# Attention and routed experts on one core: other batch groups, a closer pace of indirect DMAs, and a counted clock that goes on behind the last quad

## The chip, the cores and the metric

The kernel runs on one core of one Trainium2 chip. The core has five engines that each work through an instruction queue of their own, in order: TensorE (PE, matmuls; PEld is its weight load), VectorE (DVE), ScalarE (ACT), GpSimd (POOL) and SyncE (SP), which here only issues DMAs. The metric is the device time of the core in microseconds (us); less is faster.

## The reference, cut to what matters

One transformer block with adaptive layer norms, over 16 batches of 512 tokens of width 128, in float32:

```python
h = layernorm(x) * (1 + ca) + sa            # per batch, from L0_c
x = x + ga * attention(h)                   # 16 heads of 8, rotary, causal softmax, projection
h = layernorm(x) * (1 + cb) + sb
logits = h @ router_w.T + expert_bias       # 160 experts
top_w, top_idx = top_k(sigmoid(logits), 8)  # 8 of 160 experts a token, weights scaled to sum 2.5
routed = sum over the 8: top_w * (silu(h @ w_gate[e].T) @ w_down[e].T)
shared = silu(h @ w_gate_shared.T) @ w_down_shared.T
x = x + gb * (routed + shared)
```

So 8,192 tokens each go to 8 of 160 small experts (128 to 64 to 128).

## The kernel before, in words

**Two stages.** The first stage (`attend`, L1076, 64 head groups `gg`: 16 batches with 4 groups of 4 heads) does the attention. Beside it run, batch by batch, the preparation of a later batch (`prepare`, `rotate` L284, `values`), the projection, and the routing (`route` L519: layer norm, logits, top 8). The second stage runs the experts in *quads*.

**Groups of batches.** Batches are routed in groups, `GROUPS` (L36). When all batches of a group are routed, `place` (L601) counts how many of its tokens each pair of experts gets and gives every token and expert choice a slot in a table `xg` of that group in HBM. A group of b batches has 32b + 80 blocks of 128 slots, that is 8b + 20 quads of four blocks. The last 8 of them (6 for a group of one batch) are spare: they run inside a condition (`spare_quads`, L867) that every engine reads and that is false here. So 8b + 12 quads run for b > 1 and 22 for b = 1, 228 in all with the groups of before.

**Scatter and gather.** The token rows go into `xg` by indirect DMAs that POOL issues (`scattering`, L741): 32 a batch, 512 in all, each moving 128 rows of 512 bytes. A quad (`Quad`, L769) loads four blocks of `xg`, turns them on PE (`turn`), multiplies by the gate weights (`up`, after ACT and DVE copied them to `wq`), applies Silu on ACT (`su`), multiplies by the down weights (`down`) and writes `yg`. When all quads of a group are through, its results can be fetched back: `gathering` (L966) issues 32 indirect DMAs a batch, 512 in all, eight to a tile `got`; `combine` (L986) weighs and adds the eight rows on DVE and, at the end of a batch, sends the rows to `out`. Before a batch can be combined, `shared_expert` (L885) and `weights` (L919) must have run for it.

**What sets the order.** The kernel writes the order of every engine's queue by hand, by a *counted clock* (`Steps`, L1237). Each matmul adds its estimated time to `steps.now` (`mm`, `turned`); DVE and ACT work is followed beside it. Side work is a list of generators with due times; `steps.tick()` runs up to two steps that are due. A step that yields `LATER` comes back 3 counted us later. Nothing of this exists on the chip: it only decides in which order instructions enter the queues.

- Beside the attention, a `Pacer` (L1014) is called after each of the 14 items of a head group and lets one scatter into the queue for every `PACE` counted us, as long as a placed group has scatters left; it may catch up by four.
- In the loop over quads, `RATE` is added to `owed` at every turn, and as many indirect DMAs are issued, scatters first, then gathers. If there is none to issue, `owed` is set to 0.
- `paced` (L228) makes every indirect DMA wait for the PE instruction that was last in the order, and keeps POOL's own order.
- Behind the loop, the gathers that are left are issued one after the other (L1208). `add_up(2)` takes the results up as they are complete; if the shared expert or the weights of that batch are not there, it runs steps and moves the clock on until they are.

**What shares POOL's and SP's queues.** POOL does two elementwise steps for each of the two `rotate` calls of a batch and two for its shifted rows (`side`, L234), in the same queue as the indirect DMAs. In `rotate`, ACT's copy of the second part (L307) reads what POOL wrote, and SP's DMAs `parts<-three` (L316) wait for POOL's second step; `rows<-h` (L598) waits for POOL's steps on `h`. On SP's queue the same order also holds the rows `qrep<-mT` (L412) that each head group's scores need, the loads `krep`, `qrep` for a head group four ahead, and DMAs that clear `xg` and the spare part of `yg` (`clear`, L508); what is left of those at the end of the attention is issued ahead of the first quad's loads.

Of the kernel before, what the change touches and what calls it, by code (L numbers as in the profile page):

```python
# [32 lines left out]
E = 160  # L33
I = 64
NC = E * I // P
GROUPS = (2, 3, 3, 2, 2, 2, 1, 1)  # L36
TOPK = 8
FAR = 1e30
LAG = 3


PACE, RATE = 1.3, 2.3


AFTER, LATER, AHEAD, SLACK = 0.8, 3.0, 3.0, 3.0
# [7 lines left out]
def slot_blocks(batches):  # L53

    return TOPK * NBLK * batches + NC


NKM = slot_blocks(max(GROUPS))

# [11 lines left out]
def block_kernel(ctx: ExitStack, tc: tile.TileContext, t: dict, out: bass.AP):  # L71
# [22 lines left out]
    steps = Steps()  # L94
# [396 lines left out]

    somes = const.tile([1, len(GROUPS)], I32, tag="somes", name="somes")

    class Group:
        def __init__(self, g):
            self.g, self.size, self.first = g, GROUPS[g], sum(GROUPS[:g])
            self.tb = NBLK * self.size
            self.nk = slot_blocks(self.size)
            self.nq = self.nk // 4
            self.idx = sb.tile([P, self.tb, TOPK], I32, tag=f"idx{g}", name="idx")  # L500
            self.pid = sb.tile([1, self.nq, 9], I32, tag=f"pid{g}", name="pid")
            self.some = somes[:, g : g + 1]
            self.m, self.before = [], []
            self.hide = tc.dram_tile([2, self.nk * P], BF, name=f"hide{g}")
            self.xg = tc.dram_tile([self.nk * P, D], FP, name=f"xg{g}")
            self.yg = tc.dram_tile([self.nk * P, D], FP, name=f"yg{g}")
# [12 lines left out]
    def route(gr, i):  # L519
# [37 lines left out]
        for j in range(NBLK):  # L557
# [7 lines left out]
            if j % 2:  # L565
                yield
        m = sb.tile([P, NBLK, E], BF, tag="m", name="m", bufs=max(GROUPS) + 2)
        vec.tensor_scalar(m, marked, 0.0, None, ALU.is_gt)
# [3 lines left out]

        before = sb.tile([P, E], BF, tag="before", name="before", bufs=max(GROUPS) + 3)
        if i == 0:
            vec.memset(before, 0.0)
            gr.before.append(before)
            before = sb.tile([P, E], BF, tag="before", name="before", bufs=max(GROUPS) + 3)
        two = sb.tile([P, 2, E], BF, tag="two", name="two")
# [429 lines left out]
    def stream(*sources):  # L1008

        return next((s for s in map(next, sources) if s is not None), None)  # L1010
# [149 lines left out]
    def prepare_sums():  # L1160

        nonlocal shared_last, gathered_last
        if gathers:
            gathered_last = gathers[0][0].first + gathers[0][1]
        if shares and shares[0] <= gathered_last + 1 and (
            shared_last is None or shared_last in residual
        ):
            shared_last = shares.popleft()
            steps.add(1, shared_expert(shared_last))

    def add_up(most):
        while len(sums) > most:
            b = sums[0][0].first + sums[0][1]
            while b not in residual or residual[b][2] is None:
                prepare_sums()
                if not steps.tick():
                    steps.skip()
            combine(*sums.popleft())

    for i in range(-3, len(quads) + 5):  # L1180
# [25 lines left out]
            owed = owed - 1.0 if stream(scatter, gather) is not None else 0.0  # L1206
        add_up(LAG)
    while stream(gather) is not None:  # L1208
        steps.tick()
        add_up(2)  # L1210
        prepare_sums()
# [217 lines left out]
```

## Time and profile before

| what | value |
|---|---|
| median of 6 runs | 1999.51 us (1989.74 to 2006.53) |
| the profiled execution | 2014.3 us, span of its instructions 2012.5 us |
| PE busy | 1631.9 us, 81% of the span |
| DVE, ACT, POOL busy | 1181.6, 1080.5, 1143.7 us |
| scatters (`xg<-hs`) | 512, mean 970 ns |
| gathers (`got<-yg`) | 512, mean 1005 ns |
| attention: first issue of a scatter to last | 277.6 to 1284.8 us (the last 128 of them beside the quads) |
| quads: first and last result copy `y<-down` on ACT | 1035.9 and 1848.8 us |

The profile is one execution. Its page gives the busy time of every engine, 40 slices of the span with the busy share in tenths, the granted clock of PE, the chain of work that ended last, the costliest groups of instructions, and the DMA issues. Further answers of the trace are groups by tile, waits ("who waited for whom: us in total, times, longest"), the instructions in order of time, and the busy time of the engines in chosen windows. In waits a "q" behind an engine's name is its sequencer, and "issue" means that nothing else was waited for.

### The profile page before, as it was taken

The numbers are of one execution on the slowest core, as the hardware profiler recorded it, in microseconds if no ns is written. First come the engines' busy times: TensorE is split into PE (matmuls) and PEld (weight loads), VectorE is DVE, ScalarE is ACT, GpSimd is POOL, SyncE is SP. The second block draws the span as 40 slices with busy tenths as digits, with TensorE's granted clock in tenths as the row PEclk, the third lists the DMA queues.
The fourth block names the chain that finished last, engine by engine and source line by source line (L and its number), as shares of the span: only waits on it lengthen the run. The fifth ranks groups of instructions, "written<-read, shape, count | busy, mean of one in ns | idle before, by whom it ended". The sixth has DMA issues, their size and how long they took to land. (4 is left out here: it accounts for less than half of the span.)

```text
span 2012.5 us, 39282 instructions
## 1 busy us (share of the span) xinstructions
PE 1631.9 (81%) x12248; PEld 1117.0 (56%) x12248; DVE 1181.6 (59%) x3153; ACT 1080.5 (54%) x2031; POOL 1143.7 (57%) x1139
## 2 busy tenths in 40 slices
PE   2799999989999989898978899898888897987100
PEld 1455555555455545454457788776767776776000
DVE  2677777878777768777523324345555554455544
ACT  1366656656565545555656666565656565664000
POOL 4001147407773767776435576666666665666776
PEclk8799999999999989999989999989999898998555
DMA  3465656656675776767788899888888897987221
GB/s 88 115 185 179 183 170 208 201 170 198 201 229 177 228 218 210 229 202 227 254 269 281 264 311 311 277 279 283 286 282 278 271 303 247 301 294 234 85 67 54
DMA packets 298149, 445.30 MB, mean 221 GB/s; under 512 B 44923, under 2 KB 168796, under 8 KB 297920
## 3 DMA queue, kind: packets, MB, share of 16 engines
q1 hardware_dynamic: 265152, 375.32, 57.7%
q0 software_dynamic: 32768, 67.17, 11.5%
q8 instruction: 113, 1.85, 0.4%
q14 instruction: 116, 0.95, 0.1%
HBM read 223.37 MB, written 218.17 MB: 219 GB/s over the span
## 5 line engine op out<-in xcount | busy, mean ns | idle before, releaser
L974 POOL DMA_INDIRECT got<-yg,idx x512 | 514.5, 1005 | 262.9 <-issue 104.8
L751 POOL DMA_INDIRECT xg<-hs,idx x512 | 496.4, 970 | 273.7 <-PE s L104 111.5
L1232 DVE TENSOR_REDUCE mins<-s 128x2 f32<-128x1024 f32 (+3 forms) x448 | 396.1, 912 | 146.1 <-PE s L104 144.0
L1232 ACT ACTIVATE pT<-s 128x1024 f32<-128x1024 f32 x320 | 322.0, 1021 | 198.7 <-PE s L104 195.3
L104 PE MATMUL down<-wd,su 128*128 x1824 | 276.0, 297 | 32.6 <-ACT su L1232 10.1
L104 PEld LDWEIGHTS down<-wd,su 128*128 128x128 f32 x1824 | 232.3, 199 | 110.5 <-issue 44.6
L104 PE MATMUL up<-xT,wq 128*128 128x128 f32 x1824 | 256.7, 287 | 1.8 <-ACT xT L1232 1.8
L1232 DVE COPY wq<-wg 128x128 f32 x456 | 91.5, 252 | 257.4 <-PE up L104 183.7
L104 PEld LDWEIGHTS up<-xT,wq 128*128 128x128 f32 x1824 | 237.9, 204 | 1.9 <-issue 1.9
L1232 ACT COPY y<-down 128x512 f32<-128x512 f32 x228 | 133.8, 587 | 182.0 <-PE down L104 108.7
L104 PE MATMUL s<-krep,qrep 96*128 96x512 bf16 (+3 forms) x1024 | 198.9, 307 | 34.4 <-DMA qrep<-parts 22.2
L104 PE MATMUL s<-qrep,krep 128*128 128x512 bf16 (+3 forms) x1024 | 195.5, 304 | 34.9 <-ACT pT L1232 16.3
L104 PE MATMUL av<-pT,v 128*32 128x512 f32 (+3 forms) x2048 | 196.7, 451 | 0.0
L236 POOL TENSOR_TENSOR rot<-rot,three 128x512 f32<-128x512 f32 x32 | 36.7, 1161 | 273.7 <-ACT three L1232 273.4
L111 PE MATMUL turn<-ident,xs 128*128 128x128 f32 x912 | 148.7, 289 | 31.0 <-DMA xs<-xg 29.9
L104 PEld LDWEIGHTS <-identb 128*128 128x128 bf16 x1280 | 121.9, 99 | 84.6 <-issue 6.7
L1232 ACT ACTIVATE su<-up 128x512 f32<-128x512 f32 x228 | 136.4, 598 | 49.1 <-PE up L104 48.4
L104 PEld LDWEIGHTS <-qrep 96*128 96x128 bf16 x1024 | 82.5, 99 | 135.1 <-issue 100.1
L1232 ACT COPY xT<-turn 128x512 f32<-128x512 f32 x228 | 131.9, 579 | 27.3 <-issue 14.7
L111 PEld LDWEIGHTS turn<-ident,xs 128*128 128x128 f32 x912 | 112.3, 149 | 47.6 <-issue 29.0
L1232 ACT COPY wq<-wg 128x128 f32 x456 | 113.4, 296 | 43.1 <-issue 14.8
L104 PEld LDWEIGHTS <-krep 128*128 128x128 bf16 x1024 | 86.4, 98 | 77.8 <-issue 56.8
(174 smaller groups left out, 2202.1 us busy)
## 6 DMA issues: line engine op xcount, KB each, us to landing
xg<-zeros SPq DMA_DIRECT2D x288, 256.0 KB
xs<-xg SPq DMA_DIRECT2D x228, 256.0 KB
wd<-in_wdT SPq DMA_DIRECT2D x228, 256.0 KB
yg<-y SPq DMA_DIRECT2D x228, 256.0 KB
krep<-parts SPq DMA_DIRECT2D x64, 288.0 KB
qrep<-parts SPq DMA_DIRECT2D x192, 96.0 KB
yg<-zeros SPq DMA_DIRECT2D x60, 256.0 KB
parts<-three SPq DMA_DIRECT2D x96, 128.0 KB
```

The source lines that it names most:

```text
L104: steps.last = nc.tensor.matmul(out_, lhsT=lhsT, rhs=rhs, start=start, stop=stop).ins
L111: steps.last = nc.tensor.transpose(out_, in_, ident).ins
L236: in_order(getattr(nc.gpsimd, op)(*args).ins)
L751: s = nc.gpsimd.indirect_dma_start(out=gr.xg, out_offset=bass.IndirectOffsetOnAxis(ap=gr.idx[:, NBLK * i + j, k : k + 1], axis=0), in_=h[: ...
L974: s = nc.gpsimd.indirect_dma_start(out=got[:, k, :], out_offset=None, in_=gr.yg, in_offset=bass.IndirectOffsetOnAxis(ap=gr.idx[:, NBLK * i ...
L1232: return getattr(self.engine, op)(*args, **kwargs)
```

## The change

Four numbers change, and one line is added. The groups become 3, 3, 3, 2, 2, 1, 1, 1; the pace of the scatters beside the attention goes from 1.3 to 1.05 counted us; the indirect DMAs per turn of the quad loop go from 2.3 to 2.4; and behind the loop every gather now moves the counted clock on by 1.25, so that side steps become due between the gathers. From this follow other counts: 230 quads run instead of 228 (36 for each group of three batches, 28 for two, 22 for one), and 58 instead of 60 spare quads are cleared in `yg`.

```diff
-GROUPS = (2, 3, 3, 2, 2, 2, 1, 1)
+GROUPS = (3, 3, 3, 2, 2, 1, 1, 1)
...
-PACE, RATE = 1.3, 2.3
+PACE, RATE = 1.05, 2.4
+PERIOD = 1.25
...
     while stream(gather) is not None:
+        steps.work(PERIOD)
         steps.tick()
         add_up(2)
         prepare_sums()
```

Every line behind the numbers stands one or two lines lower in the changed kernel.

## The prediction

> **What bounds the kernel now.** I read the page's slices first, then windows by stage, then who waits for whom in each stage. The slices show two stages in which PE is nearly full, and an end in which POOL alone works:
>
> ```profile
> span 2012.5 us, 39282 instructions
> PE   2799999989999989898978899898888897987100
> POOL 4001147407773767776435576666666665666776
> PEclk8799999999999989999989999989999898998555
> ```
>
> The windows put numbers on it (PE, PEld, DVE, ACT and POOL busy, granted clock, DMA share, GB/s):
>
> ```profile
> 150.00:200.00 50.00, 47.74 (x396) 26.71 (x395) 37.84 (x81) 32.92 (x50) 7.09 (x6) 1.00 0.60 184
> 550.00:600.00 50.00, 46.79 (x382) 25.52 (x375) 36.84 (x81) 32.26 (x48) 37.53 (x37) 1.00 0.73 221
> 1600.00:1650.00 50.00, 45.73 (x331) 38.66 (x330) 26.69 (x77) 32.97 (x78) 35.00 (x36) 0.97 0.92 299
> 1950.00:2000.00 50.00, 0.00 (x0) 0.00 (x0) 23.46 (x53) 0.00 (x0) 38.12 (x40) 0.50 0.19 57
> ```
>
> Attention (to about 1001 us) and quads (to 1849) are PE's: 46 to 48 of 50 us. What POOL does there is hidden as long as nobody waits for it. The last 160 us are POOL's: 40 gathers in 50 us. The reader should see there that POOL has no hole to be filled; one gather follows the other every 1.25 us, and its waits from 1845 us on are issue time only:
>
> ```profile
> 1946.62 0.94 POOL L974 DMA_INDIRECT got<-yg,idx  x1 [0.30 <-issue]
> 1947.86 0.94 POOL L974 DMA_INDIRECT got<-yg,idx  x1 [0.30 <-issue]
> ...
> POOL got L974 <- issue: 33.8, 111, 0.3
> ```
>
> Beside the attention POOL has to serve two customers, and before the change it manages. The rows are the scatters of one group of three batches alone, all of POOL in the same window, and, from the waits of 60 to 1000 us, the wait of ACT for POOL's step in `rotate`:
>
> ```profile
> 455.00:603.00 148.00, 93.01 (x96) 0.99 0.68 211
> ...
> 455.00:603.00 148.00, 112.25 (x112) 0.99 0.68 211
> ...
> ACT three L1232 <- POOL rot L236: 2.5, 3, 1.4
> ```
>
> **The change part by part.** Sums are against the profiled span of 2012.5 us (2014.3 us in all, which is 0.7% above the median of 1999.51). A change below 0.5%, 10 us, is about what a measurement cannot tell from none.
>
> *Two quads more (36+36+36+28+28+22+22+22 = 230).* PE's part of a quad in the chain is 1.21 (up) + 1.09 (down) + 0.85 (turn) = 3.15 us. From the first to the last `y` copy, 1035.9 to 1848.8, a quad took 3.58 with the group ends, whose number does not change. Two cost 6.3 to 7.2; I take 7, PE being the bound.
>
> *The end.* In the order of POOL's instructions, 116 gathers stand behind the last group's condition before, 97 after. At 1.25 us that is 19 x 1.25 = -23.8 us. Some gathers beside the window's DVE work took up to 1.92; over the end the mean was 1.29, so the ends are -23.8 and -24.5. Why they are fewer: following the counted clock through the code, 397 instead of 384 scatters lie ahead of the end of the attention. Between there and the last condition lie 128 + 396 = 524 indirect DMAs before and 115 + 415 = 530 after: 2.30 a quad both times. The rate of 2.4 is eaten by turns that find nothing to issue while the 36 quads of the first group run, so the quads themselves carry no denser DMAs, and their pace should stay.
>
> *The clock behind the loop.* POOL waits for nothing in the end, so moving steps between the gathers can win nothing there: 0. It could lose: each gather waits for the PE instruction last in the order, now a shared-expert matmul that waits for `hr`, whose load stands on SP behind `out`, which waits for DVE. The nearest row, gathers waiting for such matmuls while quads still ran, was 41.0 us over 23 times, 6.2 the longest. Two batches are still to come there (14 and 15, one fewer than before): 0 to 12; I take 0, since their loads are issued 20 or more gathers (25 us) ahead of need or while quads run.
>
> *One more shared expert inside the quad loop* (batch 13, before in the end): PE runs of 1.00 and 1.08 us for its `o` matmuls in the chain, plus four transposes and one gate matmul: 0 to 4, I take 2.5.
>
> *Clears.* Ahead of the first quad's loads, SP issued 36 clears in 27.11 us, 0.75 each, and PE stood 16.4 us for them. Now 34: -1.5, or 0 if another load is last. The DMAs they move past are only those loads.
>
> *The closer pace.* In the window of 148 us, 96 scatters came every 1.54 us at 1.3 counted us, so a counted us is 1.19 us and the new pace asks for one every 1.25. POOL needs 0.96 + 0.30 = 1.26 for a scatter, and its side steps took 112.25 - 93.01 = 19.2 us in 148, 0.13 a us. For a group of three batches: asked in 96 x 1.25 = 120 us, needed 96 x 1.26 + 120 x 0.13 = 137. POOL falls 17 us behind by the end of the group; at the old pace, 148 against 121 + 19 = 140, it does not. Queued behind the scatters on POOL are the side steps: in the new order two `rot` steps behind 53 scatters of each large group (lag 9.4) and two behind all 96 (lag 17). ACT's copy of `three` stands 3 counted us later (3.6 us), so it holds ACT's queue, exponentials included, for 9.4 - 3.6 = 5.8 and 17 - 3.6 = 13.4 us; `parts<-three` and `rows<-h` hold SP's, and with it the `qrep<-mT` rows of the next head group. Those rows were issued 7 to 10 us ahead of their use mostly (344.37 for matmuls at 352.19). I take the near end of that margin, 7 us, as the cover of both: the first hold is hidden, the second costs 13.4 - 7 = 6.4, for three large groups 19. Bounds: 0 (all hidden) and 3 x 13.4 = 40. The next group has 64 scatters and a lag of 64/96 x 17 = 11; less 3.6 and 7 it costs nothing.
>
> A hold has a price behind it. PE stood 3.56 us at 357.0 and then ran at half clock:
>
> ```profile
> 354.00:358.00 4.00, 1.00 (x8) 0.99 0.72 210
> 358.00:361.00 3.00, 3.00 (x26) 0.50 0.56 166
> ```
>
> The clock record has 3.4 us for that stretch, so 1.7 us lost; for three holds 5 (0 to 10).
>
> The scatters' own row has a median of 960, a mean of 970 and a maximum of 1572 ns, beside a DVE that is busy 37 of 50 us. [...] By the row the stretch is 10 ns each, so the measurement decides, and the sum has nothing for it.
>
> *Sum:* 7 - 23.8 + 0 + 2.5 - 1.5 + 19 + 5 = +8.2 us on 2012.5. On the median: 1999.5 + 8 = 2008.
>
> **The rivals.**
>
> *The holds stay hidden.* For it: ACT is idle 18 of 50 us beside the attention, PE has three score banks ahead, and all its waits for `pT` come to 20.7 us in 918. Then 19 + 5 fall away: -15.8, 1984. Against it: ACT's queue is in order, and 13.4 us is more than three banks' exponentials of 1.02 us each.
>
> *The holds cost in full*, the mechanism that ends clearly slower: a lag of 17 with no cover but the 3.6 us. Three times 13.4 and 5 of half clock: 40 + 5 - 15.8 = +29, 2028. It decides from 3.6 us a group on, where 3 x 3.6 + 5 = 15.8 balances what is won; 0.5% slower needs 7. For it: the margin of `qrep<-mT` was 5.3 us in some head groups, and each lag hits ACT and SP one after the other. Against it: while PE stands, no scatter is released, so the lag stops growing.
>
> *The change does not do what it says.* The rate is no denser, as shown; if the pace too gave nothing (POOL saturated: scatters simply late), the end would still have the 97 gathers, since the order is fixed. What is left of this rival is that the scatters land as before and hold nobody: the hidden case again, with more or less of the 13 scatters' 13 x 1.25 = 16 us kept, 1984 to 2000.
>
> **How the numbers follow.** Partly covered holds (the sum) 0.50, own range -2 to +20 us, 1997 to 2019, about half of it above +10; hidden 0.22; full 0.25; the last 0.03. Predicted 2008. The range reaches from the hidden case to the full one, 1984 to 2028, and leaves out less than 2 in 10. Faster by over 0.5%: nearly all of the hidden case, 0.21. Slower by over 0.5%: the full case and almost half of the sum's, 0.48. Same: 0.31.
>
> **What would show it.** Holds: ACT `three` waiting for POOL `rot` for 20 us or more instead of 2.5, SP `parts` and `rows` for POOL too, PE gaps above 3 us with half clock behind them near the end of each large group's scatters, and the attention's end near 1025 instead of 1001. If the wait is there and the attention still ends by 1005, the first rival is right. The end: 97 gathers, last `y` copy to the end of the span near 139 us instead of 163 (2012.5 - 1849.4), POOL still without waits. Quads: 3.58 us each as before. Wrong would make it: gathers waiting for `o` matmuls in the end, another pace of the quads, or a clock that differs over a whole stage.

## The result and the profile after

The changed kernel took 2022.95 us (median of 20 runs) against 1998.21 us for the kernel before (46 runs): a ratio of 1.0116, 95% interval [1.0100, 1.0132]. The forecast was 2008 with a range from 1984 to 2028. Slower was right and the range held it, but the time lost is 25 us on the medians, three times the 8 us forecast.

Four experiments (e1 to e4) ran on a chip on which the kernel before takes 2205 us, all others on chips on which it takes 1996 to 2005; so every ratio below is to runs of the kernel before on the same chip. There is no profile of the kernel before on the slower chip; for its stages e1 to e4 are compared with each other.

The stages, read from the first and last exponential (`pT`) and the first and last `y` copy of each trace, in us. "Again" are the two kernels once more, both on one chip (e8 and e5):

| stage | before | after | before again | after again | forecast of the change |
|---|---|---|---|---|---|
| start to first `pT` | 81.9 | 81.3 | 82.6 | 82.3 | 0 |
| attention | 919.0 | 951.4 | 920.0 | 952.2 | +24 |
| last `pT` to first `y` | 35.6 | 44.4 | 37.9 | 39.7 | -1.5 |
| first to last `y` | 812.9 | 813.4 | 800.6 | 813.9 | +9.5 |
| last `y` to the end | 163.1 | 135.3 | 163.2 | 133.7 | -23.8 |
| span | 2012.5 | 2025.8 | 2004.4 | 2021.8 | +8.2 |

The slices of the changed kernel: the right end of PE's row is 9, 4, 0, 0 where it was 7, 1, 0, 0, and in the attention (slices 8 to 19) it has 8s and a 7 where mostly 9s stood. GpSimd (POOL) shows 7s there with valleys of 1 and 2 between the runs of scatters:

```profile
span 2025.8 us, 39393 instructions
PE   2799999887988898988949989988998989889400
POOL 4001114772577177775462546667666766566776
PEclk8899999998999999998978989989898989899655
```

The windows that answer to those of before (PE, PEld, DVE, ACT and POOL busy, granted clock, DMA share, GB/s). A stretch without scatters is as full as it was (47.74 of 50 us of PE); 550 to 600, in the middle of a large group's scatters, falls from 46.79 to 42.80. The quads and the end are what they were:

```profile
150.00:200.00 50.00, 47.74 (x411) 27.10 (x410) 38.16 (x91) 34.82 (x52) 7.09 (x6) 1.00 0.58 181
550.00:600.00 50.00, 42.80 (x335) 23.93 (x333) 35.58 (x88) 27.49 (x43) 39.20 (x41) 0.99 0.63 200
1600.00:1650.00 50.00, 45.59 (x331) 38.80 (x330) 30.87 (x85) 32.88 (x78) 37.91 (x38) 0.97 0.94 308
1950.00:2000.00 50.00, 0.00 (x0) 0.00 (x0) 20.46 (x47) 0.00 (x0) 37.77 (x40) 0.50 0.20 58
```

The 96 scatters of a large group now take 136 us instead of 148; the prediction worked out 137 as what GpSimd needs. The scatters alone in that window:

```profile
327.00:463.00 136.00, 92.98 (x96) 0.97 0.64 203
```

and all engines in it, where GpSimd's 106.79 us hold 13.8 of other steps:

```profile
327.00:463.00 136.00, 116.92 (x943) 64.09 (x942) 95.19 (x235) 74.25 (x113) 106.79 (x108) 0.97 0.64 203
```

And ACT stands for GpSimd's step of `rotate`: 46.4 us in 11 waits, 8.3 the longest, where it was 2.5 in 3 (waits from 60 us to the attention's end; total, times, longest):

```profile
ACT three L1234 <- POOL rot L237: 46.4, 11, 8.3
```

One of these holds in the timeline (start, duration; in brackets the idle time before it and what ended it). GpSimd comes from a scatter straight into the two `rot` steps; between them ACT gets the input it had waited 8.34 us for; behind that copy in ACT's queue stood `hT`, and PE waited 7.54 us for it:

```profile
460.23 0.96 POOL L752 DMA_INDIRECT xg<-hs,idx  x1 [0.30 <-issue]
461.21 2.27 POOL L237 TENSOR_TENSOR rot<-rot,three 128x512 f32<-128x512 f32 x2
462.40 0.62 ACT L1234 CAST three<-rot 128x512 bf16<-128x512 f32 x1 [8.34 <-POOL rot L237]
462.93 0.77 ACT L1234 ACTIVATE hT<-s,mod 128x512 f32<-128x512 f32 x1
...
463.75 1.01 PE L105 MATMUL s<-qrep,krep 128*128 128x128 bf16 x4 [7.54 <-ACT hT L1234]
```

The price behind it: PE was empty from 460 to 463, and then nearly full, but at half clock; the clock record has it until 476.5.

```profile
460.00:463.00 3.00, 0.00 (x0) 0.00 (x0) 0.00 (x0) 0.59 (x2) 2.75 (x3) 0.50 0.13 44
463.70:467.00 3.30, 3.25 (x20) 1.61 (x19) 0.49 (x1) 2.26 (x5) 3.22 (x3) 0.50 0.34 110
467.00:470.00 3.00, 3.00 (x16) 1.64 (x8) 0.80 (x2) 0.58 (x1) 1.25 (x2) 0.50 0.43 146
470.00:474.00 4.00, 4.00 (x17) 2.31 (x17) 0.79 (x1) 1.53 (x2) 0.00 (x0) 0.50 0.00 0
```

A hold of the group of two batches behind the three large ones, for which the prediction had no cost, with the copy 6.42 us late and PE's gap of 5.28 us behind it:

```profile
918.52 0.62 ACT L1234 CAST three<-rot 128x512 bf16<-128x512 f32 x1 [6.42 <-POOL rot L237]
...
919.46 0.90 PE L105 MATMUL s<-wroutT,hT 128*128 128x160 f32 x2 [5.28 <-ACT row L1234]
```

Over the attention PE's idle time went from 73.0 to 97.2 us and the time at half clock from 33.7 to 61.4 (again: 76.2 to 94.4, and 37.5 to 71.7). In the kernel before, eight `up` matmuls took 1.06 us at full clock and 1.91 at half (starting at 1307.99 and 1325.51 us); from that, half of the time in which PE is busy at half clock is put down as its cost, an estimate. PE was busy at it for 31.9 us before and 47.7 after, so 7.9 more (again 35.8 and 63.7, 14.0 more). Idle time and half clock together make 32.1 and 32.2 us, all of what the attention grew.

The end has 100 gathers behind the last `y` instead of 119, on average 1.27 us apart where it was 1.30, and GpSimd still waits for little but issue (3.2 us in 10 other waits):

```profile
POOL got L975 <- issue: 26.5, 87, 0.3
```

### The profile page after: what moved, and what is told of

It is laid out like the page before. It is cut to its first block, busy times and chain, and to the rows that moved or that the text cites. A ratio compares the mean times of both kernels' runs of the same rounds, so it can differ in the third digit from the quotient of the medians.

```text
span 2025.8 us, 39393 instructions
## 1 busy us (share of the span) xinstructions
PE 1646.2 (81%) x12289; PEld 1123.9 (55%) x12289; DVE 1171.5 (58%) x3156; ACT 1084.1 (54%) x2041; POOL 1137.4 (56%) x1139
## 3 DMA queue, kind: packets, MB, share of 16 engines
q8 instruction: 113, 1.85, 0.4%
## 5 line engine op out<-in xcount | busy, mean ns | idle before, releaser
L105 PE MATMUL down<-wd,su 128*128 x1840 | 277.3, 296 | 31.1 <-ACT su L1234 10.2
L237 POOL TENSOR_TENSOR rot<-rot,three 128x512 f32<-128x512 f32 x32 | 36.5, 1158 | 322.1 <-ACT three L1234 322.0
L1234 ACT ACTIVATE su<-up 128x512 f32<-128x512 f32 x230 | 137.6, 598 | 48.9 <-PE up L105 48.2
L1234 ACT COPY wq<-wg 128x128 f32 x460 | 114.6, 295 | 49.3 <-issue 13.8
```

Of the source, the lines that this page charges most:

```text
L105: steps.last = nc.tensor.matmul(out_, lhsT=lhsT, rhs=rhs, start=start, stop=stop).ins
L237: in_order(getattr(nc.gpsimd, op)(*args).ins)
L1234: return getattr(self.engine, op)(*args, **kwargs)
```

## The experiments

### One part alone, and the change without its pace

e1 is the changed kernel with one part undone; e2, e3 and e4 are the kernel before with one part of the change each.

```
e1, from the changed kernel          e2, from the kernel before
-PACE, RATE = 1.05, 2.4              -PACE, RATE = 1.3, 2.3
+PACE, RATE = 1.3, 2.4               +PACE, RATE = 1.05, 2.3

e3, from the kernel before           e4, from the kernel before
-PACE, RATE = 1.3, 2.3               -GROUPS = (2, 3, 3, 2, 2, 2, 1, 1)
+PACE, RATE = 1.3, 2.4               +GROUPS = (3, 3, 3, 2, 2, 1, 1, 1)
```

> The changed kernel with only the pace of the scatters put back to 1.3 counted us; groups 3,3,3,2,2,1,1,1, rate 2.4 and the counted clock behind the loop stay. Theory of the holds (scatters in POOL's queue hold the side steps that ACT and SP wait for): ACT's wait for POOL in rotate falls from 46.4 us to 3 or less, the attention ends at about 1001 instead of 1033 us, PE idle in it near 73 instead of 97 us, the end stays at 135 us: 1970 to 1985 us, 1 to 1.4% under the kernel before. Rival, the groups (a first group of three batches starts its scatters a batch later and moves routing work): the attention stays near 1030 and the time at 2015 to 2025.

> The kernel before with only the pace changed, 1.05 for 1.3 counted us. Theory of the holds: two large groups and two or three of 64 scatters fall within the attention; holds of ACT by POOL of 30 to 45 us in all, attention longer by 20 to 32 us, the end unchanged at 160 us or so: 2018 to 2030 us, 1.0 to 1.6% slower. Rival, the groups: no more than 5 us from 1998. Rival, denser scatters slow PE through the DMA queues and not through waits: slower by as much, but with ACT waiting for POOL under 5 us.

> The kernel before with only the rate changed, 2.4 for 2.3 indirect DMAs a turn of the quad loop. If the rate is what shortens the end: the order of instructions leaves about 21 gathers fewer behind the last condition, 21 x 1.25 = 26 us, quads unchanged: 1970 to 1975 us, 1.2 to 1.4% faster. If the prediction's reading is right, that the rate is eaten by empty turns and the pace fills the end: within 8 us of 1998. Rival, denser gathers beside the quads slow them: the end shorter by 26 us, the quads longer by as much, 1998.

> The kernel before with only the groups changed to 3,3,3,2,2,1,1,1. Two quads more at 3.5 us, the end unchanged or some gathers longer because the first gathers start later, no holds (ACT waiting for POOL in rotate 3 us or less): 1998 to 2012 us, same to 0.7% slower. If the groups carry the loss, 2018 or more, with the attention longer by 20 us or the first quad's loads later by 9 us as in the changed kernel.

| run | median us | ratio to before | 95% interval | attention | gathers behind the last `y` |
|---|---|---|---|---|---|
| e1 changed, pace 1.3 | 2200.22 | 0.9992 | [0.9964, 1.0020] | 1025.7 | 97 |
| e2 pace alone | 2263.83 | 1.0277 | [1.0223, 1.0331] | 1086.0 | 117 |
| e3 rate alone | 2193.07 | 0.9952 | [0.9927, 0.9977] | 1020.8 | 94 |
| e4 groups alone | 2212.52 | 1.0041 | [1.0012, 1.0069] | 1021.6 | 117 |

So on this chip the loss lies in the pace: alone it costs 2.8%, and without it the changed kernel is level with the one before. And the rate is not without effect, as the prediction had it: with the rate alone 94 gathers are left for the end, with pace or groups alone 117 (the kernel before leaves 119 on the other chips).

What e2 did not show was the wait. With a pace of 1.05 and the old groups, on this chip, ACT's wait for `rot` (60 to 1170 us) is the old one, and yet the attention is 65 us longer than in e3 and e4 (against e3, 31.5 us of PE's idle time and 35 of half clock):

```profile
ACT three L1232 <- POOL rot L236: 2.5, 3, 1.4
```

So a second theory had to be tested: that scatters in close succession slow the attention themselves, whoever waits for GpSimd.

### Both kernels again, ACT's copy later, the pace alone

e5 is the changed kernel and e8 the kernel before, unchanged; e7 is e2's kernel again; e6 is the changed kernel with this edit in `rotate`, so that ACT's next copy is put 4 counted us later into its queue:

```
-        yield side("tensor_tensor", r, r, three[:, 0, :], ALU.subtract)
+        yield side("tensor_tensor", r, r, three[:, 0, :], ALU.subtract) + 4.0
```

> The changed kernel once more, so that it stands beside its variants on one chip. If the parts of the change simply add up as the runs so far had them (pace +2.8%, rate -0.5%, groups +0.4%), 1.027 of the kernel before on a chip that runs the kernel before in 2205 us, and 1.012 on one that runs it in 1998 us.

> The changed kernel with ACT's first copy of three issued 4 counted us later behind POOL's step of rotate; the same scatters at the same pace. Theory A, the closer pace costs by ACT's queue being held for POOL's late steps: ACT's wait of three for POOL's rot falls from 46 us to below 20, PE's gaps of 5 to 8 us behind it go, and the attention is 15 to 30 us shorter than in the changed kernel, the time 0.988 to 0.995 of it. Theory B, scatters in close succession slow the attention whoever waits for POOL: the wait falls as well, but the attention keeps its length within 8 us, and the time stays within 0.4% of the changed kernel.

> The kernel before with the pace of 1.05 alone, once more, beside a profile of the kernel before on the same chip. There was no wait of three for POOL's rot in it, so by theory A (only the holds cost) it is within 0.5% of the kernel before on a chip where the kernel before takes 2000 us; by theory B it is 2% or more slower there too, as it was at 1.028 on the slower chip, with 15 us or more of PE's waits that are not for POOL.

> The kernel before, for its profile on this chip. If it is the chip of 2205 us, the blocks of four heads that have no scatters beside them take 51 and 53 us as on the first chip, and those with 35 to 42 scatters take 66 to 76 instead of 56 to 69; on the first chip the profile repeats itself within 1%.

| run | median us | ratio to before | 95% interval | attention | PE idle in it | half clock in it |
|---|---|---|---|---|---|---|
| e5 changed | 2021.67 | 1.0126 | [1.0094, 1.0159] | 952.2 | 94.4 | 71.7 |
| e6 changed, copy later | 2018.95 | 1.0117 | [1.0086, 1.0148] | 948.1 | 96.3 | 51.0 |
| e7 pace alone | 2028.33 | 1.0159 | [1.0122, 1.0196] | 946.3 | 91.7 | 64.8 |
| e8 before | 2006.2 (one run) | | | 920.0 | 76.2 | 37.5 |

On this chip the pace alone does make ACT wait, so the statement in e7's expectation that there was no such wait holds for the slower chip only. ACT's wait in e7 (60 to 1030 us):

```profile
ACT three L1232 <- POOL rot L236: 33.1, 10, 6.7
```

and two of PE's (81 to 1028 us), for tiles that stand behind `three` in ACT's queue; e8 has 0.6 us for `hT` and none for `row`:

```profile
PE s L104 <- ACT row L1232: 8.2, 2, 5.6
PE s L104 <- ACT hT L1232: 6.1, 3, 5.4
```

e6 is the instructive one. The edit does what it says: ACT's wait for GpSimd is back at 2.5 us. Yet the attention is only 4.1 us shorter than in e5 and the time 0.1% less. Theory A (the holds of ACT are the cost) wanted 15 to 30 us. What PE waited for in e6 (82 to 1030 us):

```profile
PE s L105 <- DVE mins L1234: 26.2, 47, 1.9
PE s L105 <- DMA qrep<-mT: 17.1, 7, 3.9
PE s L105 <- ACT pT L1234: 13.4, 24, 2.2
PE o L112 <- DVE hide L1234: 8.2, 9, 1.6
PE s L105 <- DMA qrep<-parts: 6.4, 3, 4.0
```

The waits for `pT`, `hT` and `row` went down from 48.9 us in e5 to 13.4; in their place PE waits 23.5 us for rows of the next head group (`qrep`, by DMA; 10.4 in e5, 4.5 in e8) and 26.2 for VectorE's `mins` (7.9 in e5, but 19.3 in e8 too). By this run alone, theory B has it: the time is B's. But there is a third reading, A2: what is late is GpSimd's step, and whichever way that lateness is passed on, through ACT's queue or through rows that the rest of the chain makes late, PE ends up waiting for it. One such chain stands in e6's timeline: behind its scatters GpSimd comes late to its steps on `h`, SP's `rows<-h` waits 10.0 us for them, the `qrep` rows stand right behind it on SP, and PE waits for these:

```profile
930.83 2.62 POOL L237 TENSOR_TENSOR h<-h,row 128x512 f32<-128x512 f32 x2
...
933.47 0.34 SPq L599 DMA_DIRECT2D rows<-h  x1
933.91 0.77 SPq L413 DMA_DIRECT2D qrep<-mT  x1
...
936.22 0.61 PE L105 MATMUL s<-qrep,krep 128*128 128x512 bf16 x1 [3.91 <-DMA qrep<-mT]
```

The lateness itself can be read in the trace, as the time from ACT's copy that feeds a `rot` step to the step's start: 12.1 to 15.3 us for 11 of the 13 late steps in the changed kernel (the other two 8.2 and 9.3), 6.4 to 11.4 for most in e6, at most 8.8 in e8.

### GpSimd's steps on VectorE

This separates A2 from B: scatters as close as before, but nothing of `rotate` behind them. In e9, e10 and e13, `side` (the two subtractions of `rotate` and the two steps on rows) is VectorE's:

```
 def side(op, *args):
-    in_order(getattr(nc.gpsimd, op)(*args).ins)
+    getattr(nc.vector, op)(*args)
     return LATER
```

e9 is the kernel before with this, e10 also has the pace of 1.05. e11 and e12 are the kernel before with one number changed:

```
e11                                  e12
-PACE, RATE = 1.3, 2.3               -PACE, RATE = 1.3, 2.3
+PACE, RATE = 1.2, 2.3               +PACE, RATE = 1.3, 2.6
```

> The kernel before with the two subtractions of rotate and the two steps on rows done by VectorE instead of GpSimd, so that nothing but indirect DMAs stands in GpSimd's queue beside the attention; pace 1.3. It is the base for the next run. Some 96 steps of about 0.65 us go to a DVE that is busy 37 of 50 us: 0.995 to 1.01 of the kernel before by either theory.

> The same with the pace of 1.05: scatters as close as in the changed kernel, but no step of rotate can be late behind them. Theory A2, the closer pace costs because GpSimd's steps of rotate come late (whether ACT is held by them or the rows of the next head group arrive late): within 0.4% of e9, attention within 8 us of e9's. Theory B, close scatters slow the attention themselves: 1.2% or more above e9, attention 20 us or more longer.

> The kernel before with pace 1.2 instead of 1.3. By the working of the prediction a scatter is then asked every 1.43 us, a group of 96 in 137 us, and GpSimd needs 121 + 18 = 139, so the queue lags by 2 us only. Theory A2: ACT's wait of three for rot stays below 8 us and the time is within 0.4% of the kernel before. Theory B, a cost in proportion to the density: 40% of what pace 1.05 cost (1.0159), that is 1.006.

> The kernel before with 2.6 indirect DMAs a quad. If the rate is not eaten by turns without work (as the 94 instead of 117 gathers behind the last quad at 2.4 had it), there are 50 to 60 gathers behind the last quad, and the end is shorter by 60 x 1.25 = 75 us; quads get denser indirect DMAs (2.6 x 1.26 = 3.28 us of GpSimd in a quad of 3.5) and may lose some of it again: 0.965 to 0.985. If gathers then wait for rows that the quads have yet to write, or quads slow down by more than 0.2 us each, 0.99 or more.

| run | median us | ratio to before | 95% interval | attention | PE idle in it |
|---|---|---|---|---|---|
| e9 before, side steps on VectorE | 2001.91 | 0.9976 | [0.9951, 1.0002] | 920.5 | 79.3 |
| e10 the same, pace 1.05 | 2001.81 | 1.0005 | [0.9983, 1.0028] | 917.3 | 78.7 |
| e11 before, pace 1.2 | 2013.83 | 1.0037 | [1.0013, 1.0062] | 933.2 | 81.1 |
| e12 before, rate 2.6 | 1933.21 | 0.9661 | [0.9625, 0.9697] | 917.5 | 75.8 |

e10 settles it for these chips. The scatters are as dense as in the changed kernel, 62 in 80 us or one every 1.29 us, beside a VectorE that is busy 63.79 of them (window of e10, scatters alone):

```profile
465.00:545.00 80.00, 59.62 (x62) 0.96 0.66 206
```

(and all engines in it):

```profile
465.00:545.00 80.00, 70.42 (x549) 38.60 (x552) 63.79 (x169) 43.62 (x64) 59.62 (x62) 0.96 0.66 206
```

and they cost nothing that the attention shows: 917.3 us against 920.5 in e9, medians level, ratios 0.3% apart. Theory B wanted 20 us or more and falls; A2 stands. PE's longest rows of waits in e10 (80 to 997 us) are those of the kernel before (20.4, 10.1, 4.9 and 19.3 us in e8, in this order), without a hold and without late rows (`qrep` 1.9 us against 4.5 in e8):

```profile
PE s L104 <- ACT pT L1232: 29.3, 34, 2.8
PE o L111 <- DVE hide L1232: 12.1, 11, 2.7
PE s L111 <- DVE ms L1232: 7.8, 8, 2.8
PE s L104 <- DVE mins L1232: 7.7, 19, 1.4
```

e11 does not decide by itself, and its profile is of an execution that took 2025 us, 0.6% above its median. ACT's wait is 2.5 us, as A2 expects, but the `rot` steps are up to 7.6 us late rather than the 2 worked out (in e8 up to 8.8, so the longest is no longer), the attention is 13 us longer than e8's (5 of PE's idle time, 8 by half clock), and 1.0037 lies between A2's bound of 0.4% and B's 1.006, with an interval that touches both.

e12 was meant as a test of the rate, and became the first version that is clearly faster than both kernels: 54 gathers behind the last `y` instead of 119, 79.5 us from there to the end instead of 163, while the quads took 808.5 us, within what they take in the kernel before (800.6 and 812.9). Its slices show GpSimd denser in the quads and the empty right end of PE nearly gone:

```profile
span 1922.9 us, 39205 instructions
PE   2799998999989998988978889988887998988930
POOL 4001126614774676777634667677776776777776
```

### What is left of the change without the late steps

e13 is the changed kernel with `side` on VectorE. e14 is the kernel before with the counted clock going on behind the loop:

```
 while stream(gather) is not None:
+    steps.work(PERIOD)
     steps.tick()
```

e15 is e10 with `RATE` 2.8, e16 is e13 with `RATE` 2.8.

> The changed kernel with rotate's subtractions and the steps on rows on VectorE. Theory A2 (the pace costs by GpSimd's late steps alone): the attention is back within 8 us of the kernel before, and what is left is groups, rate, clock and 13 scatters more in the attention: by the prediction's sum without holds -15.8 us, 0.992 of the kernel before; by the runs of single parts (rate -0.5%, groups +0.4%) 0.997 to 0.999. Were the late steps not the cause within the changed kernel, it stays above 1.008.

> The kernel before with the counted clock going on by 1.25 us at each turn behind the last quad, alone. By the prediction 0 with a bound of +12 us, since GpSimd waits for nothing in the end: 0.998 to 1.002. If gathers wait for late shared-expert matmuls, up to 1.006 and waits of GpSimd for PE of several us behind the last y.

> The kernel before with pace 1.05, rate 2.8 and the side steps on VectorE. The rate leaves some 25 to 40 gathers behind the last quad instead of 54 at 2.6: 20 to 35 us less than 0.966, so 0.950 to 0.960, if the quads carry the denser gathers (2.8 x 1.26 = 3.5 us of GpSimd a quad, all of a quad's time); if they can't, quads slow down and it is 0.960 to 0.970.

> The changed kernel with rate 2.8 and the side steps on VectorE: as e15 with groups 3, 3, 3, 2, 2, 1, 1, 1 and the clock behind the loop. Two quads more and a longer start (+0.4%) against 13 scatters more beside the attention, which are worth nothing where the quads' end is already empty: 0.3 to 0.6% above e15. If the smaller last groups let more gathers pass before the last quad, it is level with e15 or below.

| run | median us | ratio to before | 95% interval | attention | gathers behind the last `y` |
|---|---|---|---|---|---|
| e13 changed, side steps on VectorE | 1997.59 | 0.9957 | [0.9927, 0.9987] | 927.5 | 99 |
| e14 clock behind the loop alone | 2001.70 | 0.9991 | [0.9967, 1.0016] | 923.5 | 119 |
| e15 before, pace 1.05, rate 2.8, side steps on VectorE | 1914.98 | 0.9568 | [0.9522, 0.9614] | 915.2 | 32 |
| e16 changed, rate 2.8, side steps on VectorE | 1928.79 | 0.9621 | [0.9574, 0.9668] | 929.7 | 35 |

Moving six small steps a batch to another engine turns the change from +1.26% to -0.43%. The attention, 927.5 us, is some 8 us above the kernel before, at the edge of what A2 expected, and far from the 951 of the change. The clock behind the loop is worth nothing, as forecast. The parts add up on these chips: the pace alone 1.0159, all the rest, if e13 is taken for it, 0.9957, together 1.0116 against 1.0126 measured.

With a higher rate the new groups lose: e16 is 0.5% above e15 by the ratios. The end has nearly the same number of gathers in both, and what the new grouping costs remains. Its attention is 14.5 us longer; e13's is 10.2 us longer than e10's. e15, the old groups with the pace, the rate and the moved steps, is the best version found: 4.3% faster than the kernel before. Its slices have PE full to the last but one:

```profile
span 1907.7 us, 39119 instructions
PE   2799998999889889989987889988889888889870
```

## Why the prediction was right and wrong

**The closer pace: mechanism right, size too small.** The holds came where they were put: GpSimd's two `rot` steps behind the scatters of each large group, ACT's queue held, PE empty, half clock behind. The sum had 19 for the holds and 5 for half clock, 24 in all; the attention grew by 32.4 and 32.2 us in the two pairs. PE's idle time took 24.2 and 18.2 of it, near the 19. The rest, 8.2 and 14.0, is the clock, against 5: PE's additional work at half clock cost 7.9 and 14.0. The prediction had priced one stretch of 3.4 us behind each of three holds; the gap of 7.54 us came with a stretch of 17 us (459 to 476), and the one of 5.28 us with 10.2 (917 to 927).

**The step that failed is the cover, and with it the price of the clock.** The prediction had lags of 9.4 and 17 us, a first hold of 5.8 hidden under 7 us of margin, a second of 13.4 that costs 6.4, and for the next group, of two batches, a cost of nothing. In the trace the lag is nearly the same at both places of the first two groups, 12 to 15 us; ACT's holds were 6.0 and 8.3 for the first large group, 7.3 and 8.3 for the second, 4.9 and 1.6 for the third, and 6.4 for the group of two. The first hold was about the size forecast but not hidden: PE stood 2.36 us behind it, and 3.62 in the second group. Of the second, 8.3, PE stood for 7.54. Behind the third group's holds there is no gap above 2.04 us, and the hold of the group of two cost PE 5.28. So the margin of the `qrep` rows did not cover ACT's queue: tiles that PE needs at once (`pT`, `hT`, `row`) stand in it. That the idle time came near the 19 is partly luck: the holds in all were smaller than the prediction's, but less of them was covered, and a group counted at nothing took the place of one that cost little. e6 shows that the margin of the rows is not free either: ACT stands 2.5 us for GpSimd instead of 40.9 in e5, and PE waits 23.5 us for the rows instead of 10.4.

**The new grouping in the attention was not in the sum.** With no late steps, e13's attention is still 10.2 us longer than e10's: PE's idle time is 3.8 us longer (waits for `qrep` rows of 8.2 us against 1.9), and half clock costs 8.0 more. The difference sits in the last two batches, which take 104.9 us against 92.0; in e13 scatters run beside them to the end, in e10 they end 27 us ahead of it. At the old pace, on the slower chip, the groups alone show no such cost (1021.6 us in e4, 1020.8 in e3). How much of the changed kernel's 32 us is the grouping's is not settled.

**The end: size a little low, cause wrong.** 19 gathers fewer were forecast, 19 or 20 came, and the end shrank by 27.8 and 29.5 us, not 23.8: besides, the gathers came 1.27 and 1.26 us apart instead of 1.30, which is another 3 to 4 us; why, was not traced. But the prediction said that the rate of 2.4 is eaten and that 13 scatters moved into the attention do it. e1, the changed kernel at the old pace, has 386 scatters started when the attention ends, against 384 with the old groups, and 97 gathers behind the last `y` all the same (the changed kernel: 390 and 100). e3 has the rate alone leave 94; e2, e4 and e7, pace or groups alone, leave 117 to 119. The equal count of 2.30 a quad was an average over two unlike parts: between the end of the attention and the first group's last `y`, its 36 quads carry 70 indirect DMAs, 1.9 a quad, with stretches of 28 and 36 us in which none is issued, and the others 2.4 (67 in the 28 quads of a group of two, against 64 before).

**Quads and start.** From first to last `y` the sum had +9.5. The two pairs differ by 0.5 and 13.3. Over all runs with the old groups at a rate of 2.3 on these chips (812.9, 800.6, 798.3, 806.3, 796.4, 808.0, 801.3) the mean is 803, over those with the new groups at 2.4 (813.4, 813.9, 809.6, 819.5) it is 814: +11, so the term came near, and the profile that the prediction was read from was a slow one in just this stage. The start of the quads, forecast at -1.5, was 8.8 and 1.8 longer: fewer clears stand ahead of the first loads (32 in 29.80 us against 36 in 27.11), but they took longer.

**Profile and median.** The stages give the +13.3 and +17.4 us by which the spans of the two pairs differ. The sum was short by 8 in the attention and by 3 to 10 in the start of the quads, and too high by 4 to 6 at the end. The medians differ by 25. The kernel before was 0.8% and 0.5% above its median in its two profiled runs, the changed kernel 0.2% and 0.1%; so some 10 of the 17 us by which the forecast fell short lie between the profiled execution and the median and in no term of the sum. With the +11 of the mean over the runs for the quads, the stages alone come to some 15 to 24 us.

**The rivals.** The measured 2023 lies above the 1997 to 2019 that the prediction gave its own case; that the wider range held it is owed to the full case, 2028. "The holds stay hidden" is out, by the 46.4 us and the attention's end at 1033. "The holds cost in full" had 2028 and is nearer to 2023 than the forecast, for reasons that its text did not have: the holds were shorter than 13.4, but the short ones counted too, the clock behind them cost more than 5, and part of the difference is that of profile and median. "The change does not do what it says" is out.

## What stays open

On the slower chip the pace cost 2.8%, with the `rot` steps at most 5.6 us late and no hold of ACT. That is not explained by the mechanism shown here, and the version with the side steps on VectorE was not run there. Nor is it explained why e11's attention was 13 us longer, where the `rot` steps are as late as in the kernel before and no later: a part of the pace's price may lie outside the late steps, but e10 bounds it, at the full pace, to what its ratio of 1.0005 against 0.9976 leaves.

## What to carry to other kernels

Here GpSimd took 136 us for 96 scatters that were asked for in an estimated 120 (96 x 1.25), and 11 of its 13 late `rot` steps came 12.1 to 15.3 us late. Where a queue is asked for more than it can do, look for the small steps that share it and ask who waits for them, before asking whether its own work is dense enough. Price what comes behind a wait as well: here half clock behind PE's gaps took 8 and 14 of the attention's 32 us. If a wait is taken away at one engine and the time stays, look at whether the same lateness now arrives by another path (e6), and test the cause by moving the late work elsewhere (e10). An average such as 2.30 a quad can hide two opposite changes: count by group before calling a parameter idle.

## What the runs showed of the hardware

The same step costs GpSimd and VectorE differently: the subtraction of two 128x512 f32 tiles took 1158 ns on GpSimd in the changed kernel and 681 ns on VectorE in e10:

```profile
L237 POOL TENSOR_TENSOR rot<-rot,three 128x512 f32<-128x512 f32 x32 | 36.5, 1158 | 322.1 <-ACT three L1234 322.0
```

```profile
L236 DVE TENSOR_TENSOR rot<-rot,three 128x512 f32<-128x512 f32 x32 | 21.0, 681 | 0.2
```

That is 1.7 times, and what the move was worth lay not in the 0.48 us a step (at the old pace it brought 0.9976 in e9) but in the queue that the step left.

Scatters at one in 1.29 us took 977 ns on average in e10, against 970 at one in 1.54 us before: with their own density and a busier VectorE together (63.79 of 80 us in the window of e10, 74.74 of 100 at 635 to 735 us of the kernel before) they were 7 ns longer.

TensorE fell to half clock behind gaps of 3.62, 2.04 and even 1.85 us (ending at 598.5, 867.8 and 902.6 us of the changed kernel) and stayed there for 3.4 us each time; a gap of 2.36 us (402.4) brought none. With the gap of 7.54 us it was at half clock from 459 to 476 us. Why a gap of 1.85 us was followed by half clock and one of 2.36 us was not, no run shows.

On the slower chip the time was lost where indirect DMAs run: the two batches without scatters beside them took 51.4 and 53.1 us on both kinds of chip, while the attention as a whole was 101 us longer in e3 than in e8, the quads 74 us and the end 23 us longer in e2 than in e8, which have the same groups and rate. A scatter took 967 ns in e3 against 968 in e8. What stands out is TensorE idle with nothing in the profile that it waits for. In e3 (81 to 1102 us):

```profile
PE s L104 <- issue: 46.4, 38, 5.8
```

and in e8 (81 to 1003 us):

```profile
PE s L104 <- issue: 0.7, 3, 0.2
```

No run here tells what that is.
